# Three casts to ScalarE, ten transposes fewer and another form of one addition, in a graph-attention and quantised-FFN kernel

## The chip, the core and the metric

The kernel runs on one core of a Trainium2 chip. The core has TensorE (PE, matrix products), VectorE (DVE), ScalarE (ACT) and GpSimd (POOL), and SyncE (SP), which here only issues DMAs. PEld is TensorE's weight load, which runs beside its products. The metric is the time of one execution in microseconds of the device; smaller is better. Before the change it is 374.53 us, the median of three runs (374.22 to 374.98).

## What is computed

The input x has 384 rows (nodes) of 1024 features. Two residual blocks follow one another:

```
y = layernorm(x)
q, k, v   = y Wq' + bq,  y Wk' + bk,  y Wv' + bv            1024 x 1024 each
q2,k2,v2  = q Wiq' + biq, k Wik' + bik, v Wiv' + biv        16 heads of 64
mask[s,d] = softplus(edge weight of the edge's type), -inf where there is no edge
attn      = softmax(q2 k2' / 8 + mask)                       per head, 384 x 384
x = x + (attn v2) Wo' + bo

xq   = fake_quant(layernorm(x))          one scale from the largest magnitude
gate = xq quant(Wgate)'                  352 x 1024, a scale for each row
up   = xq quant(Wup)'
h    = fake_quant(silu(gate) * up)       one scale from the largest magnitude
x = x + h quant(Wdown)'                  1024 x 352, a scale for each row
```

quant and fake_quant divide by a scale, round to whole numbers from -128 to 127 and multiply by the scale again. The kernel keeps the whole numbers in bfloat16, multiplies those, and puts the scales back afterwards. The graph-attention block is in float32.

## The kernel before

**Stages.** The span has five parts, by the profile's time. To about 23 us: the layer norm, and the first q blocks. To about 162: the q, k, v and inner-q projections. To about 325: the attention over 8 pairs of heads, with the inner-k and inner-v projections and the quantisation of the FFN weights filled in between. To about 348: the output projection's end, the residual and the second layer norm. Then the FFN.

**The projections.** The weights come in blocks of 128 output features, 512 KB each, two blocks at a time (a pair of blocks, wa and wb, in `project2`). A pair is computed with seven products on halves instead of eight (Strassen's scheme). Each product is `product` (L190), whose four float32 matmuls are eight records in the profile. Around them VectorE makes sums of weights before the products (`left_sums`: L170 s1, L172 s2, L174 the first half of wb; L211, in place, half of wa) and combines the results (L201, L207, L218, L219, L222); ScalarE has two steps for each pair (L204, a copy, and L214, which adds a bias). The second product needs s2 (L172), the sixth needs L211, and a product needs a PSUM buffer that the steps of an earlier one have read out: of four in the projections, of two (`ps_mm`) in the first inner-k pair.

**The mask.** While the projections run, VectorE finds repeated edges (L424 and L431 to L434) and GpSimd scatters the edge values into the mask in DRAM by indirect DMA (L437), four chunks at a time.

**The FFN weights.** `ffn_weights` takes the weights in 14 units: three gate blocks (128, 128 and 96 rows of 1024), three up blocks of the same sizes, and eight down blocks (128 rows of 352). Each unit is loaded by SP (L533) into one of three `row` buffers, so a load waits until the scaling of the unit three before has read its row. `quantise_rows` then takes the row maximum (VectorE, L512), the scale (L513) and its reciprocal (L515), scales to int8 (ScalarE, L518, into the single buffer `w8b`) and casts to bfloat16 (VectorE, L520, into one of two buffers `wqi`). Later TensorE transposes the block (L550 or L557) and ScalarE copies it to its place (L551, L558, L559).

**What sets the order.** On TensorE, SP and GpSimd the order is the program's. On VectorE and ScalarE it is written out up to the end of the projections and again from the second layer norm; between, and for the FFN weights' steps, a scheduler places the instructions, and puts the first units among the projections' last steps. When an instruction waits, everything behind it on its engine waits.

**The end.** In the FFN, TensorE makes gate and up (L920) and, after them, turns the down scales (L937, eight transposes). VectorE multiplies (L927) and reduces to the largest magnitude (L930, L942). Meanwhile TensorE transposes the identity matrix 17 times (L878, in `keep_busy`; nothing reads the results). Then it turns the column of maxima (`all_max`, L129), VectorE reduces it (L131), takes the reciprocal (L948), and VectorE and ScalarE scale h to int8 (L955, L957) and VectorE casts it (L960). Six groups of three matmuls follow (L969), each read out with its scales by VectorE (L973) into y. GpSimd adds the residual x to the first three (L977), VectorE to the last three (L981), after all six are read out. SP sends each out (L978, L982), 256 KB each.

Of the kernel before, what the change touches and what calls it, by code (L numbers as in the profile page):

```python
# [28 lines left out]
ALU = mybir.AluOpType  # L29
# [6 lines left out]
F = 1024  # L36
# [25 lines left out]
def gnn_ffn_kernel(ctx: ExitStack, tc: tile.TileContext, a: dict, out: bass.AP):  # L62
    nc = tc.nc
# [19 lines left out]
    x = act.tile([P, NT, F], F32, name="actT")  # L83
# [50 lines left out]
    w_scale = ffn.tile([P, 2, 3], F32)  # L134
# [372 lines left out]
    v2 = act.tile([P, NT, F], F32, name="actT")  # L507
    outT = act.tile([P, KC, N], F32, name="actT")

    def quantise_rows(wn, rows, n, scale):  # L510
        mx = small.tile([P, 1], F32, name="wmx")
        nc.vector.tensor_reduce(mx[:rows], wn[:rows, :n], axis=AX.X, op=ALU.max, apply_absolute_value=True)  # L512
        nc.vector.tensor_scalar(scale, mx[:rows], 1.0 / QMAX, None, op0=ALU.mult)  # L513
        rs = small.tile([P, 1], F32, name="wrs")
        nc.vector.reciprocal(rs[:rows], scale)  # L515

        w8b = rows_p.tile([P, F], I8, name="w8b", bufs=1)
        nc.scalar.activation(w8b[:rows, :n], wn[:rows, :n], AF.Copy, scale=rs[:rows])  # L518
        wq = rows_p.tile([P, F], BF16, name="wqi", bufs=2)
        nc.vector.tensor_copy(wq[:rows, :n], w8b[:rows, :n])  # L520
        return wq

    def ffn_weights():

        units = [(name, m, ic) for m, name in enumerate(("L0_ffn_w_gate", "L0_ffn_w_up")) for ic in range(3)]
        units += [("L0_ffn_w_down", 2, c) for c in range(KC)]
        ahead = []

        def load_row():
            name, m, j = units[len(ahead)]  # L530
            i0, rows = ICS[j] if m < 2 else (j * P, P)
            wn = rows_p.tile([P, F], F32, name="row")
            nc.sync.dma_start(wn[:rows, : F if m < 2 else I], a[name][i0 : i0 + rows, :])  # L533
            ahead.append(wn)

        load_row()
        load_row()
        yield
        for u, (name, m, j) in enumerate(units):
            wn = ahead[u]  # L540
            if len(ahead) < len(units):
                load_row()
            if m < 2:
                i0, rows = ICS[j]
                wT = (wgT, wuT)[m]
                wq = quantise_rows(wn, rows, F, w_scale[:rows, m, j : j + 1])
                yield
                pt = ps_tp.tile([P, KC, P], BF16, name="tp")
                for k in range(KC):
                    nc.tensor.transpose(pt[:, k, :rows], wq[:rows, k * P : (k + 1) * P], ident_b[:rows, :rows])  # L550
                nc.scalar.copy(wT[:, :, i0 : i0 + rows], pt[:, :, :rows])  # L551
            else:
                wq = quantise_rows(wn, P, I, wd_scale[:, j : j + 1])
                yield
                pt = ps_tp.tile([P, 3, P], BF16, name="tp")
                for ic, (i0, rows) in enumerate(ICS):
                    nc.tensor.transpose(pt[:rows, ic, :], wq[:, i0 : i0 + rows], ident_b)  # L557
                nc.scalar.copy(wdT[:, 0:2, j * P : (j + 1) * P], pt[:, 0:2, :])  # L558
                nc.scalar.copy(wdT[:96, 2, j * P : (j + 1) * P], pt[:96, 2, :])  # L559

    prep = ffn_weights()

    next(prep)
    nc.sync.dma_start(biv_b, row_bcast(a["L0_gnn_biv"], F))

    with ExitStack() as ph:
# [19 lines left out]
        def inner_v(c):  # L586

            cs = slice(c * 256, (c + 1) * 256)
            wt = []
            for j in range(2):  # L590
                wt.append(w.tile([P, F], F32, name="wt"))
                nc.sync.dma_start(
                    wt[j].rearrange("p (k o) -> p k o", k=HK),
                    a["wiv"][j * HK : (j + 1) * HK, :, cs].rearrange("k p o -> p k o"),
                )

            def steps():
                for t in range(NT):
                    pm = ps_mm.tile([P, 256], F32, name="mm")
                    for k in range(KC):  # L600
                        k0 = k % HK * 256
                        nc.tensor.matmul(  # L602
                            pm, vT[:, k, t * P : (t + 1) * P], wt[k // HK][:, k0 : k0 + 256],
                            start=(k == 0), stop=(k == KC - 1),
                        )
                        if k < KC - 1:
                            yield
                    nc.vector.tensor_add(v2[:, t, cs], pm, biv_b[:, cs])
                    yield

            return steps()
# [58 lines left out]
        def out_group(wo, t, g, ks, pm):  # L670
            gs = slice(g * 512, (g + 1) * 512)
            for k in ks:
                nc.tensor.matmul(  # L673
                    pm, outT[:, k, t * P : (t + 1) * P], wo[k][:, gs], start=(k == 0), stop=(k == KC - 1)
                )
                yield
# [11 lines left out]
        for p in range(NP):  # L688
# [4 lines left out]
            if p == NP - 1:  # L693
                early = [(t, g, ps_mm.tile([P, 512], F32, name="mm")) for t, g in ((0, 0), (0, 1))]
                fill, n = (s for t, g, pm in early for s in out_group(wo, t, g, range(NP - 2), pm)), 2 * (NP - 2)
            elif p % 2:
                k2_next, fill = inner_k(p + 1)
                n = 7 * HK + 1
            else:
                fill, n = inner_v(p // 2), NT * KC  # L700
            if p == NP - 2:

                x = act.tile([P, NT, F], F32, name="actT")
# [4 lines left out]
                for t in range(NT):  # L708
                    for g in range(2):
                        gs = slice(g * 512, (g + 1) * 512)  # L710
# [139 lines left out]
    with ExitStack() as ph:  # L850
        ff = ph.enter_context(tc.tile_pool(name="ff", bufs=3))
        ps_x = ph.enter_context(tc.tile_pool(name="ps_x", bufs=4, space=PSUM))
# [21 lines left out]
        def keep_busy(n, pool, name):  # L874

            pt = pool.tile([P, P], F32, name=name)
            for _ in range(n):
                nc.tensor.transpose(pt, ident, ident)  # L878
# [34 lines left out]
        for col, ic, c0, width in ((0, 0, 0, N), (1, 1, 0, N), (2, 2, 0, N // 2), (3, 2, N // 2, N // 2)):  # L913
            i0, rows = ICS[ic]
# [18 lines left out]
        for g in range(2):  # L933
# [2 lines left out]
                c = 4 * g + j  # L936
                nc.tensor.transpose(pt[:, j, :], wd_scale[:, c : c + 1].to_broadcast([P, P]), ident)  # L937
            nc.scalar.copy(wd_scale_b[:, g * 512 : (g + 1) * 512], pt.rearrange("p a b -> p (a b)"))
        keep_busy(17, ps_x, "x")
        mx = small.tile([P, 1], F32, name="hmax")  # L940
        scaled = small.tile([P, 4], F32, name="hscaled")
        nc.vector.tensor_tensor_reduce(  # L942
# [18 lines left out]
        last = []  # L961
        for t in range(NT):
            ts = slice(t * P, (t + 1) * P)
            for g in range(2):
                gs = slice(g * 512, (g + 1) * 512)
# [6 lines left out]
                y = ff.tile([P, 512], F32, name="y", bufs=6)  # L972
# [4 lines left out]
                    nc.gpsimd.tensor_add(y, x[:, t, gs], y)  # L977
                    nc.sync.dma_start(out[t * P : (t + 1) * P, gs], y)  # L978

        for t, gs, y in last:  # L980
            nc.vector.tensor_add(y, x[:, t, gs], y)  # L981
            nc.sync.dma_start(out[t * P : (t + 1) * P, gs], y)  # L982


# [45 lines left out]
```

## Time and profile before

| | |
|---|---|
| median of three runs | 374.53 us (374.22 to 374.98) |
| the profiled execution's own time | 375.57 us |
| its span, first to last instruction | 372.7 us |
| mean granted clock of TensorE | 0.995 |
| TensorE busy | 359.5 us, 96% |
| VectorE busy | 257.1 us, 69% |
| ScalarE busy | 115.5 us, 31% |
| GpSimd busy | 76.0 us, 20% |

A line of the timeline gives the start, the length, the engine, the line in the code, the operation, the output and the inputs, the count, and in square brackets how long the engine was idle before it and what it waited for. Pipelined instructions overlap a little, so the pitch from one start to the next is shorter than the length shown. A line of the stretches ("139.50:164.50") gives the length of the stretch, the busy time of TensorE, its weight load, VectorE, ScalarE and GpSimd, each with a count, then the granted clock of TensorE, the busy share of the DMA engines, and GB/s.

### The profile page before, as it was taken

To read this page: it belongs to the slowest core of one execution; us is meant where nothing else is said; L and a number is where in the kernel's file an instruction comes from. 1 tells how busy PE (TensorE), PEld (TensorE's weight loads), DVE (VectorE), ACT (ScalarE), POOL (GpSimd) and SP (SyncE) were. 2 spreads that over 40 slices of the span, in tenths; PEclk is the share of its full clock that TensorE was granted. 3 is DMA by queue.
4 is the path that set the end of the run, shared out by engine and by line. 5 is a ranking of instruction groups with operands and counts; after the bars stand their busy time and mean duration, and the time that the engine had idled before them with its cause. 6 is when DMAs were issued, how large, how long until landed. Compare 5 with 4: busy or idle time off the path is not lost.

```text
span 372.7 us, 5875 instructions
## 1 busy us (share of the span) xinstructions
PE 359.5 (96%) x2112; PEld 299.9 (80%) x2113; DVE 257.1 (69%) x785; ACT 115.5 (31%) x275; POOL 76.0 (20%) x81
## 2 busy tenths in 40 slices
PE   8999999999999999989999999999999999999981
PEld 8999999999999998888887868686866545449660
DVE  5788878888889969986497357717492621099665
ACT  2352110000000003023482556445444533033630
POOL 6010355455444543430000000000000000000003
PEclk9999999999999999999999999999999999999998
DMA  7969333443333377551170040050294000000004
GB/s 234 393 249 371 130 115 113 116 134 115 113 113 115 113 267 224 176 152 68 38 233 15 19 133 20 21 170 0 96 381 130 36 0 2 0 0 4 0 0 169
DMA packets 17804, 44.50 MB, mean 119 GB/s; under 512 B 3262, under 2 KB 8400, under 8 KB 17392
## 3 DMA queue, kind: packets, MB, share of 16 engines
q1 hardware_dynamic: 15104, 39.46, 31.4%
q0 software_dynamic: 2672, 4.68, 3.9%
q8 instruction: 16, 0.26, 0.3%
q14 instruction: 12, 0.10, 0.1%
HBM read 41.91 MB, written 2.21 MB: 118 GB/s over the span
## 4 chain that ended last, share of the span: by engine, by line
PE 76%; DVE 16%; DMA 3%; ACT 2%; issue 1%; DVEq 0%; POOL 0%; POOLq 0%; ACTq 0%
PE p L190 33%; PE mm L190 8%; PE mm L602 8%; PE tp L655 4%; PE sc L625 3%; PE sc L663 3%; PE mm L673 3%; PE sc L673 3%; PE mm L307 3%; DMA row<-in_L_ffn_w_down_dram 3%; PE tp L315 2%; DVE wmx L512 1%; DVE e L645 1%; DVE st L774 1%; PE mm L920 1%
## 5 line engine op out<-in xcount | busy, mean ns | idle before, releaser
L437 POOL DMA_INDIRECT mask_d<-value,place x51 | 60.5, 1186 | 65.2 <-DVE place L434 45.9
L190 PE MATMUL p<-actT,wt 128*128 128x192 f32 x360 | 66.2, 327 | 1.0 <-DVE wt L211 1.0
L190 PEld LDWEIGHTS p<-actT,wt 128*128 128x128 f32 x360 | 59.5, 190 | 1.8 <-DVE wt L211 1.5
L602 PE MATMUL mm<-wt,actT 128*128 128x256 f32 x192 | 46.1, 384 | 0.0
L602 PEld LDWEIGHTS mm<-wt,actT 128*128 128x128 f32 x192 | 34.8, 190 | 7.8 <-issue 2.2
L635 ACT ACTIVATE e<-s,mn 128x384 f32<-128x384 f32 x48 | 29.0, 605 | 28.2 <-DVE mn L631 28.1
L631 DVE CUSTOM_DVE_ANT_0 s<-sc,mask 128x384 f32<-128x384 f32 x48 | 24.4, 552 | 15.0 <-PE sc L625 14.9
L190 PE MATMUL p<-x_right,s 128*128 128x192 f32 x176 | 32.2, 326 | 0.0
L190 PE MATMUL p<-x_right,wt 128*128 128x192 f32 x176 | 32.2, 326 | 0.0
L855 POOL MEMSET hT<- 128x384 f32 x1 | 0.4, 418 | 154.7 <-PE sc L663 154.7
L190 PEld LDWEIGHTS p<-x_right,s 128*128 128x128 f32 x176 | 29.2, 190 | 0.0
L190 PEld LDWEIGHTS p<-x_right,wt 128*128 128x128 f32 x176 | 29.2, 190 | 0.0
L657 ACT COPY eTs<-tp 128x384 f32<-128x384 f32 x48 | 20.5, 478 | 25.3 <-PE tp L655 25.3
L424 DVE SCALAR_TENSOR_TENSOR junk<-key_b,key,later 128x384 f32<-128x384 f32 (+3 forms) x51 | 27.5, 539 | 0.0
L204 ACT COPY actT<-p 128x192 f32<-128x192 f32 x15 | 4.8, 321 | 64.7 <-PE p L190 64.7
L201 DVE SCALAR_TENSOR_TENSOR actT<-p,bias,actT 128x192 f32<-128x192 f32 x45 | 18.6, 414 | 7.7 <-PE p L190 4.5
L214 ACT ACTIVATE actT<-p,bias 128x192 f32<-128x192 f32 x15 | 6.3, 420 | 50.8 <-PE p L190 29.3
L655 PEld LDWEIGHTS tp<-ident,e 128*128 128x128 f32 x144 | 17.1, 141 | 4.9 <-issue 2.4
L655 PE MATMUL tp<-ident,e 128*128 128x128 f32 x144 | 19.7, 273 | 0.3 <-ACT eTs L657 0.3
L625 PE MATMUL sc<-k,actT 64*128 64x384 f32 x96 | 20.0, 519 | 0.0
L190 PE MATMUL mm<-actT,wt 128*128 128x192 f32 x96 | 19.0, 330 | 0.0
L645 DVE TENSOR_SCALAR e<-e,rs 128x384 f32<-128x384 f32 x48 | 17.2, 415 | 0.4
(220 smaller groups left out, 593.2 us busy)
## 6 DMA issues: line engine op xcount, KB each, us to landing
wt<-in_wq_dram SPq DMA_DIRECT2D x8, 512.0 KB
wt<-in_wk_dram SPq DMA_DIRECT2D x8, 512.0 KB
wt<-in_wv_dram SPq DMA_DIRECT2D x8, 512.0 KB
wt<-in_wiq_dram SPq DMA_DIRECT2D x8, 512.0 KB
wt<-in_wik_dram SPq DMA_DIRECT2D x8, 512.0 KB
wt<-in_wiv_dram SPq DMA_DIRECT2D x8, 512.0 KB
wt<-in_wo_dram SPq DMA_DIRECT2D x8, 512.0 KB
actT<-in_x_dram SPq DMA_DIRECT2D x6, 512.0 KB
```

What stands on the lines that cost most here:

```text
L190: nc.tensor.matmul(z, left[:, k * P : (k + 1) * P], r[:, k, :], start=(k == 0), stop=(k == HK - 1))
L201: nc.vector.scalar_tensor_tensor(dst, z, b, with_, op0=ALU.add, op1=ALU.add)
L424: nc.vector.scalar_tensor_tensor(junk[:, :left], keys[:, (c - k0) * P : (c - k0) * P + left], key[:, c : c + 1], later[:, :left], op0=ALU. ...
L437: ins = nc.gpsimd.indirect_dma_start(out=mask_d, out_offset=bass.IndirectOffsetOnAxis(ap=place[:, c : c + 1], axis=0), in_=value[:, c : c ...
L602: nc.tensor.matmul(pm, vT[:, k, t * P : (t + 1) * P], wt[k // HK][:, k0 : k0 + 256], start=(k == 0), stop=(k == KC - 1),)
L625: nc.tensor.matmul(ps[t, h], q2[hs, t * P : (t + 1) * P], k2[hs, :], start=True, stop=True)
L631: nc.vector.tensor_tensor_reduce(s, ps[t, h], mask[:, t, :], -SCALE, 3.0e38, op0=ALU.add, op1=ALU.min, accum_out=mn[h][:, t : t + 1],)
L635: nc.scalar.activation(e[h][:, t, :], s, AF.Exp, bias=mn[h][:, t : t + 1], scale=-1.0, accum_out=sm[h][:, t : t + 1],)
L645: nc.vector.tensor_scalar(e[h][:, t, :], e[h][:, t, :], rs[:, t : t + 1], None, op0=ALU.mult)
L655: nc.tensor.transpose(pt[:, t * P : (t + 1) * P], e[h][:, t, m * P : (m + 1) * P], ident)
L657: nc.scalar.copy(eT[h][m], pt)
L673: nc.tensor.matmul(pm, outT[:, k, t * P : (t + 1) * P], wo[k][:, gs], start=(k == 0), stop=(k == KC - 1))
```

## The change

Three edits in three places.

The casts: for the first three units, which are the three gate blocks, the cast from int8 to bfloat16 is issued on ScalarE instead of VectorE. The other eleven stay on VectorE.

The transposes of the identity matrix behind gate and up: 7 instead of 17.

The first of the three additions that VectorE makes at the end: x times 1.0 plus y in one scalar_tensor_tensor instead of a tensor_add. The values are the same.

```diff
-    def quantise_rows(wn, rows, n, scale):
+    def quantise_rows(wn, rows, n, scale, on_scalar=False):
...
         nc.scalar.activation(w8b[:rows, :n], wn[:rows, :n], AF.Copy, scale=rs[:rows])
         wq = rows_p.tile([P, F], BF16, name="wqi", bufs=2)
-        nc.vector.tensor_copy(wq[:rows, :n], w8b[:rows, :n])
+        if on_scalar:
+            nc.scalar.copy(wq[:rows, :n], w8b[:rows, :n])
+        else:
+            nc.vector.tensor_copy(wq[:rows, :n], w8b[:rows, :n])
         return wq
...
-                wq = quantise_rows(wn, rows, F, w_scale[:rows, m, j : j + 1])
+
+                wq = quantise_rows(wn, rows, F, w_scale[:rows, m, j : j + 1], on_scalar=u < 3)
...
-        keep_busy(17, ps_x, "x")
+        keep_busy(7, ps_x, "x")
...
-        for t, gs, y in last:
-            nc.vector.tensor_add(y, x[:, t, gs], y)
+        for n, (t, gs, y) in enumerate(last):
+            if n == 0:
+
+                nc.vector.scalar_tensor_tensor(y, x[:, t, gs], 1.0, y, op0=ALU.mult, op1=ALU.add)
+            else:
+                nc.vector.tensor_add(y, x[:, t, gs], y)
             nc.sync.dma_start(out[t * P : (t + 1) * P, gs], y)
```

The scheduler's order changes with it, on VectorE and ScalarE only, and only around the projections' last steps and the first units. On VectorE, the row maximum of the third gate block and that of the first up block stand earlier, both ahead of L172 of the last inner-q pair; the reciprocal of the third gate block stands ahead of that pair's L174; and the maximum of the last up block stands just ahead of L207 of the first inner-k pair instead of just behind it. On ScalarE the scaling of the third gate block moves ahead of L214 of the last inner-q pair, and its cast stands between the first wgT copy and the scaling of the first up block.

## The prediction

> **What bounds the kernel now.** I read the page first, then the timelines of TensorE, VectorE and ScalarE where the casts run, then the timeline and fine windows of the end.
>
> ```profile
> PE 359.5 (96%) x2112; PEld 299.9 (80%) x2113; DVE 257.1 (69%) x785; ACT 115.5 (31%) x275; POOL 76.0 (20%) x81
> ...
> 139.50:164.50 25.00, 23.61 (x141) 22.48 (x140) 24.78 (x68) 5.14 (x8) 10.80 (x8) 1.00 0.54 166
> ...
> 148.36 1.57 PE L190 MATMUL p<-actT,wt 128*128 128x192 f32 x8 [0.42 <-DVE wt L211]
> 152.96 1.57 PE L190 MATMUL p<-right,s 128*128 128x192 f32 x8 [0.43 <-DVE s L172]
> 158.96 1.57 PE L190 MATMUL p<-actT,wt 128*128 128x192 f32 x8 [0.53 <-DVE wt L211]
> 167.56 1.57 PE L190 MATMUL mm<-k_right,wt 128*128 128x192 f32 x8 [0.53 <-DVE k L201]
> ...
> 146.70 0.69 DVE L520 CAST wqi<-w8b 128x1024 bf16<-128x1024 int8 x1
> 148.64 0.68 DVE L520 CAST wqi<-w8b 128x1024 bf16<-128x1024 int8 x1
> 153.37 1.20 DVE L512 TENSOR_REDUCE wmx<-row 128x1 f32<-128x1024 f32 x1
> 165.96 1.22 DVE L512 TENSOR_REDUCE wmx<-row 96x1 f32<-96x1024 f32 x1 [0.82 <-DMA row<-in_L_ffn_w_up_dram]
> 160.72 1.15 ACT L518 ACTIVATE w8b<-row,wrs 96x1024 int8<-96x1024 f32 x1 [3.13 <-DVE w_scale L513]
> ...
> 357.42 2.02 PE L878 MATMUL x<-ident 128*128 128x128 f32 x17
> 358.03 0.08 DVE L942 DVE_READ_ACCUMULATOR2_ANT hmax<- 128x1 f32 x1
> 359.27 0.27 PE L129 MATMUL tp<-ident,hmax 128*128 128x128 f32 x1
> 365.27 1.26 POOL L977 TENSOR_TENSOR y<-actT,y 128x512 f32<-128x512 f32 x1
> 365.93 1.15 DVE L981 TENSOR_TENSOR y<-actT,y 128x512 f32<-128x512 f32 x1
> 367.25:367.50 0.25, 0.00 (x0) 0.00 (x0) 0.25 (x1) 0.00 (x0) 0.00 (x0) 1.00 0.43 164
> 369.75:370.00 0.25, 0.00 (x0) 0.00 (x0) 0.00 (x0) 0.00 (x0) 0.00 (x0) 0.50 0.96 385
> ```
>
> TensorE is the bound over the whole span. It lost time where the first two casts run: in the 25 us from 139.5 VectorE is busy for 24.78, and TensorE stops three times there and once just after, each time for VectorE. At the end, the 17 idle transposes run on after VectorE has the maximum ready (358.11); the next transpose, which the chain needs, stands behind them. The last addition group starts slowly: 1.15 us against 0.68 for its two neighbours, while GpSimd's third addition is still running (to 366.53). Then the DMA engines are full from about 367.35 to 370.2.
>
> **Part 1, the casts.** Three int8-to-bf16 casts (gate rows; pitch 0.61 us each on VectorE) go to ScalarE. ScalarE's price is not in the trace. The nearest rows are its 128x1024 copy (bf16, 1.01 us) and its 128x1024 scaling to int8 (1.15 us); the dearest per element, the 128x384 exponential at 0.605 us, would make 1.6 us. The low end is VectorE's own 0.68. I take 1.05, from the copy, which has the same operation and size.
>
> The order of the built program also changes on VectorE. The row maximum of the third gate block and of the first up block move earlier, to before L172 (s2) of the last wiq pair; the third reciprocal comes before that pair's L174, so the third scaling to int8 on ScalarE no longer waits until 160.72 but starts near 153.45. This frees the row buffer, and SP, with only two wik loads ahead of it (their 1 MB passed by 155 before), can fetch the last up block some 7 us sooner. That ends the 0.82 us DMA wait at 165.96.
>
> A product is eight matmul records and takes 1.30 us undisturbed. Walking VectorE's new order with the measured pitches (added values, semaphores about 0.07 us):
> - L207 to 146.10, L170 to 146.70, no cast, L201 to 147.02, L211 to 147.62. TensorE needs L211 at 147.78: the first stop goes.
> - L424 to 148.03, moved maximum (1.13) to 149.16. ScalarE meanwhile does scaling, cast, scaling, and is at L214 by 148.5 as before, so L201 runs to 149.48. L158, L218 and L513 to 150.28.
> - The second moved maximum reads the first up block. Its load is issued at 146.20 as before and its half-microsecond windows show the bytes past by 149.3, so it runs at once, to 151.41. L219, L424, L222 to 152.22, L172 to 152.82. TensorE is there already at 151.68: the second stop stays, longer, and the product starts near 152.87 instead of 152.96. Here the two saved casts (1.22) are spent on the moved maximum (1.13).
> - After it VectorE has that maximum behind it: L174 to 154.57, L201 to 157.17, L211 to 157.77. TensorE asks at 158.18: the third stop goes.
> - The second up block's maximum runs 159.51 to 160.64, the last one's 163.11 to 164.24 without a wait; L207 ends 164.51, before TensorE asks for its PSUM buffer at 164.68; L201 to 165.2, before 165.98: the fourth stop goes.
> TensorE so ends the first wik pair at 169.88 instead of 171.79.
>
> As a check: a stop costs its gap and a slow restart. Start to start, the four cost 0.69, 0.70, 0.80 and 1.03, together 3.22 us; after, one of about 1.3 is left. Gain 1.9.
>
> The third cast is off the path on VectorE (its idle before is 0.45). On ScalarE it stands behind the first wgT copy and ahead of the scaling of the first up block: that scaling ends near 179.2 instead of 180.07, since all is 1.9 earlier and the cast takes 1.05. The first w_down row then lands at 181.45 by the 2.25 us of the chain's row; the row maximum on VectorE waits for it and the next scaling ends at 182.55 instead of 184.73. Nothing TensorE needs is later than its 1.9. From there to the end TensorE is nearly dense (72.89 of 73.00 us from 195 to 268), loads are started by finished work, and the gain should carry through. ScalarE has the room: 5.14 of 25 us busy. Bounds: 0.7 (the last stop stays and the exponential's rate holds on ScalarE) to 2.3 (the small TensorE gap at 192.5 goes too). I take -1.9.
>
> **Part 2, ten transposes fewer.** Their pitch is 1.85/17 = 0.109 us, so 1.09. With seven, TensorE is free at 358.07; the maximum, read out at 358.11, reaches it near 358.17 (row_max took 0.06 earlier). The weight load of L129, at 359.16, starts there: -1.0. What is late next is VectorE's reduction chain. Behind L129 all follows at once (L131, L948, L955, L960, L969), GpSimd and the output DMAs with it. Bounds -1.09 and 0. [...]
>
> **Part 3, the addition as scalar_tensor_tensor.** Its own price is 0.06 over the plain add (0.74 against 0.68 in L973 and L981). Whether it also stands still beside GpSimd no row shows: L973, not slowed under GpSimd, reads one operand from PSUM; this one reads both from SBUF, as the slowed add does. If it runs free, VectorE ends 0.41 earlier (next start 366.59 for 367.00); if not, 0.06 later. The chain of waits would book that on the path. I book 0: from 367.35 the DMA engines carry four 256 KB blocks without a pause, some 0.7 us each, beginning with GpSimd's third, issued at 366.56. The first block from VectorE is queued behind that one on SP, and the last is already issued (368.3) while the engines still work off earlier ones. Bounds -0.2 and +0.06.
>
> [...]
>
> **Sum.** -1.9 - 1.0 + 0 = -2.9. The profiled execution took 375.57 (span 372.7 and 2.87 around it), so 372.7; it lies 1.04 above the median of the runs, 374.53, which becomes **371.6**.
>
> **Rivals.**
> - *The full list of gains*: the new form runs free and the last blocks follow it, and the gap at 192.5 goes: -1.9 - 0.15 - 1.0 - 0.2 = -3.25, 371.3. For it: the chain of waits; against: the full DMA windows. I keep it in the likeliest case's own range, 370.9 to 372.2.
> - *Half of part 1*: a row maximum moved earlier meets a row not yet landed, or ScalarE's cast takes 1.6 and delays L214 and so L201, and a stop is back. Each stop costs 0.7 to 1.0: -0.9 - 1.0 = -1.9, 372.6. Against: 1 us of slack on the landing, 0.5 on L214.
> - *The maximum is not ready*: part 2 gives only what VectorE's reduction allows, say half. -2.4, 372.1. Against: 358.11 is read from the trace.
> [...]
>
> [...]
> - *No change seen*: the path returns the time at a later wait, 374.5. Little speaks for it.
>
> **How the numbers follow.** Forecast with the first rival 0.62, half of part 1 0.14, part 2 halved 0.07, slower by clock or a wait that I don't see 0.12, none 0.05. The measurement tells about 0.2% (0.7 us) from no change. Faster 0.83, same 0.05, slower 0.12. The range takes the first three: 370.7 (all gains, less 0.2 of spread) to 373.2 (part 1 at its lower bound 0.7, part 2 whole, rounded up).
>
> **What would show it.** In the profile after: TensorE's rows with waits for L211 near 148 and 158 and for L201 near 167 gone, the one for L172 near 152.9 still there; no DMA wait at the last up maximum; the three casts on ScalarE near 1.05 us; the attention's first L602 group near 169.9; L878 x7, with the weight load of L129 right after the maximum; clock 1.00 through L969; the first last addition either 0.74 or near 1.2 us, with no difference to the end; span near 369.8. It is wrong if VectorE stops at a row maximum for a DMA, if the time gained by 170 is given back before 268, or if the clock falls before 361.

## The result, and the profile after

The changed kernel takes 371.59 us, the median of six runs (370.62 to 372.53); six runs of the kernel before beside them gave 374.29 (373.26 to 374.98). The ratio is 0.9931, with a 95% interval from 0.9913 to 0.9949: 2.6 us faster (1.9 to 3.3). The forecast was 371.6, 2.9 us below the 374.53 that three runs had given for the kernel before.

The profiled execution is the slowest of the six: 372.53 us, span 370.8 (before 375.57 and 372.7). Of the 3.04 us between the two executions 1.14 lie outside the spans (2.87 around the span before, 1.73 after) and say nothing of the change; 1.9 lie inside.

The page of the changed kernel, the stretch from 139.5 to 164.5 (columns as before), then the timeline of TensorE, ScalarE and VectorE there:

```profile
PE 357.4 (96%) x2102; PEld 298.6 (81%) x2103; DVE 255.3 (69%) x782; ACT 118.2 (32%) x278; POOL 72.7 (20%) x81
...
139.50:164.50 25.00, 23.33 (x140) 22.32 (x139) 23.91 (x68) 7.10 (x10) 7.96 (x8) 1.00 0.66 205
...
142.19 1.57 PE L190 MATMUL p<-actT,wt 128*128 128x192 f32 x8 [0.54 <-DVE actT L201]
154.35 1.57 PE L190 MATMUL p<-right,s 128*128 128x192 f32 x8 [1.01 <-DVE s L172]
...
147.61 1.04 ACT L521 CAST wqi<-w8b 128x1024 bf16<-128x1024 int8 x1
154.92 1.15 ACT L518 ACTIVATE w8b<-row,wrs 96x1024 int8<-96x1024 f32 x1 [1.23 <-DVE w_scale L513]
...
140.59 1.22 DVE L512 TENSOR_REDUCE wmx<-row 128x1 f32<-128x1024 f32 x1 [2.54 <-DMA row<-in_L_ffn_w_gate_dram]
149.44 1.21 DVE L512 TENSOR_REDUCE wmx<-row 96x1 f32<-96x1024 f32 x1
151.69 1.20 DVE L512 TENSOR_REDUCE wmx<-row 128x1 f32<-128x1024 f32 x1
153.62 0.68 DVE L172 TENSOR_TENSOR s<-s,wt 128x512 f32<-128x512 f32 x1
```

The three stops that were to go are gone, and the one for s2 is there, 1.01 long. The two row maxima moved ahead of L172 are seen just before it. The casts are on ScalarE, 1.04 us each, and the third scaling starts at 154.92 instead of 160.72. One thing was not forecast: a stop of 0.54 us at 142.19, because VectorE waited 2.54 us for the first gate row (before: 1.57, and no stop).

The end, from the timeline, and two fine windows (length, five engines, granted clock, DMA share, GB/s):

```profile
356.44 0.93 PE L882 MATMUL x<-ident 128*128 128x128 f32 x7
357.06 0.08 DVE L946 DVE_READ_ACCUMULATOR2_ANT hmax<- 128x1 f32 x1
357.26 0.13 PEld L129 LDWEIGHTS tp<-ident,hmax 128*128 128x128 f32 x1
360.85 3.72 POOL L981 TENSOR_TENSOR y<-actT,y 128x512 f32<-128x512 f32 x3 [15.20 <-DVE y L977]
363.97 1.15 DVE L987 SCALAR_TENSOR_TENSOR y<-actT,y 128x512 f32<-128x512 f32 x1
365.04 1.28 DVE L989 TENSOR_TENSOR y<-actT,y 128x512 f32<-128x512 f32 x2
...
367.50:368.00 0.50, 0.00 (x0) 0.00 (x0) 0.00 (x0) 0.00 (x0) 0.00 (x0) 0.50 0.99 373
368.00:368.50 0.50, 0.00 (x0) 0.00 (x0) 0.00 (x0) 0.00 (x0) 0.00 (x0) 0.50 0.39 143
```

L129's weight load follows the maximum by 0.12 us. The addition in its new form takes the 1.15 us that the plain one took: GpSimd's third addition runs to 364.57. The DMA engines are again full until just past 368, long after VectorE's last addition.

Ahead of the last products (L969 before, L973 after) TensorE is idle, in the kernel before from 359.54 to 361.33. Before, then after:

```profile
361.33 0.60 PE L969 MATMUL mm<-wdT,hq 128*128 128x512 bf16 x2 [1.79 <-DVE hq L960]
...
359.38 0.60 PE L973 MATMUL mm<-wdT,hq 128*128 128x512 bf16 x2 [1.79 <-DVE hq L964]
```

**A table by stage.** The profiles of the experiments can be laid beside each other by five landmarks: start of the s2 product near 133; start of the s2 product of the last inner-q pair (152.96 before); the attention's first group (L602 before); the first of the eight transposes of the down scales (L937 before); the weight load of L129; the end of the span. Each column is the time from one to the next in us.

```
                       133-s2   s2-attention   -scales    -L129    -end
before                 19.70       18.83       184.75     2.62    13.54
only the seven         19.70       18.76       184.43     1.69    13.48
only the form          19.60       18.97       184.57     2.62    13.60
only the casts         19.67       17.08       184.49     2.63    13.55
two casts              20.58       17.09       184.97     2.62    13.56
changed, first         20.66       17.09       184.13     1.69    13.54
changed, again         19.52       17.08       184.45     1.69    13.53
no transposes          20.03       17.08       184.44     1.69    13.49
operand in PSUM        19.67       17.08       184.23     1.68    13.53
two rows early         19.90       17.08       184.83     1.69    13.52
three rows early       18.97       17.09       184.41     1.69    13.52
later maxima           18.97       17.09       184.08     1.69    13.47
later, two rows        20.28       17.08       184.38     1.69    13.50
later, three rows      18.20       16.98       184.27     1.69    13.53
```

The second, fourth and fifth columns hardly move except by the edit that acts on them. The third has a scatter of 0.9. The first one moves by itself, from 19.52 to 20.66 in two executions of the same kernel, and the experiments go after it.

### The profile page after: what moved, and what is told of

The parts are those of the page before. It is cut to its first block, busy times and chain, and to the rows that moved or that the text cites. A ratio compares the mean times of both kernels' runs of the same rounds, so it can differ in the third digit from the quotient of the medians.

```text
span 370.8 us, 5857 instructions
## 1 busy us (share of the span) xinstructions
PE 357.4 (96%) x2102; PEld 298.6 (81%) x2103; DVE 255.3 (69%) x782; ACT 118.2 (32%) x278; POOL 72.7 (20%) x81
## 4 chain that ended last, share of the span: by engine, by line
PE 80%; DVE 12%; DMA 4%; issue 1%; ACT 1%; SPq 1%; DVEq 0%; ACTq 0%
PE p L190 32%; PE mm L190 10%; PE mm L606 10%; PE sc L629 5%; PE tp L659 4%; PE sc L667 4%; PE mm L677 3%; PE sc L677 3%; PE mm L307 3%; DMA wt<-in_wq_dram 3%; DMA row<-in_L_ffn_w_gate_dram 2%; DVE st L778 1%; PE mm L924 1%; DVE y L977 1%; PE x L924 1%
## 5 line engine op out<-in xcount | busy, mean ns | idle before, releaser
L437 POOL DMA_INDIRECT mask_d<-value,place x51 | 57.2, 1122 | 68.4 <-DVE place L434 47.9
L201 DVE SCALAR_TENSOR_TENSOR actT<-p,bias,actT 128x192 f32<-128x192 f32 x45 | 18.7, 415 | 7.6 <-PE p L190 4.7
L214 ACT ACTIVATE actT<-p,bias 128x192 f32<-128x192 f32 x15 | 6.3, 420 | 49.1 <-PE p L190 27.6
L612 DVE TENSOR_TENSOR actT<-mm,biv_b 128x256 f32<-128x256 f32 x12 | 5.1, 422 | 18.9 <-PE mm L606 18.8
```

Of the source, the lines that this page charges most:

```text
L201: nc.vector.scalar_tensor_tensor(dst, z, b, with_, op0=ALU.add, op1=ALU.add)
L437: ins = nc.gpsimd.indirect_dma_start(out=mask_d, out_offset=bass.IndirectOffsetOnAxis(ap=place[:, c : c + 1], axis=0), in_=value[:, c : c ...
```

## The experiments

Differences are the ratio against the kernel before on the same chip, less one, times its median (374.14 us; 374.23 for the two casts, the operand and the two kernels with three rows early), with the 95% interval in brackets. A profile is of one execution, which can lie anywhere in the spread of its kernel's runs.

**Each part alone, and the whole again.** The first kernel has only the casts' edit, the second only `keep_busy(7, ...)`, the third only the scalar_tensor_tensor.

```diff
+wq = quantise_rows(wn, rows, F, w_scale[:rows, m, j : j + 1], on_scalar=u < 3)   # first alone
+keep_busy(7, ps_x, "x")                                                          # second alone
+nc.vector.scalar_tensor_tensor(y, x[:, t, gs], 1.0, y, op0=ALU.mult, op1=ALU.add)  # third alone
```

> Only the three casts on ScalarE, with the order on VectorE that comes with it; 17 transposes and the plain addition stay. Theory of the prediction: -1.9 us beside the kernel before (range -1.2 to -2.3), because three of the four stops of TensorE between 148 and 168 us go and the one for s2 (L172) stays, about 1.2 us long. Rival (the gain is luck of landing DMAs, since the first gate row landed at different times in the two profiles): -0.5 to 0. Rival (ScalarE becomes the wait): 0 or slower.

Measured: 372.86 us, -1.2 (-1.8 to -0.6); two thirds of the -1.9. In its profile the casts do all that they were to do: only the stop for s2 is left, 1.30 long, and the attention starts at 169.63. But this execution is the fastest of the twelve (372.07), so the profile shows more gain than the median. The kernel has the casts together with the scheduler's new order; no run has the casts on ScalarE in VectorE's old order, so the two are not told apart.

> Only 7 transposes instead of 17 behind gate and up. Theory: -1.0 us; the weight load of the transpose of the maxima starts about 0.1 us after the maximum is read out, the granted clock stays 1.00 through the last matmuls. Rival (the clock falls in the idle stretch in some executions): a wider spread, some runs 2 us or more above the others, and a mean gain under 0.5 us.

Measured: 372.89 us, -1.0 (-1.5 to -0.5). The four stops stay as before, and L129's weight load stands 0.12 us behind the end of the maximum's read:

```profile
357.82 0.08 DVE L942 DVE_READ_ACCUMULATOR2_ANT hmax<- 128x1 f32 x1
358.02 0.13 PEld L129 LDWEIGHTS tp<-ident,hmax 128*128 128x128 f32 x1
```

> Only the first last addition as scalar_tensor_tensor. Theory: 0.0 us (within 0.15); the instruction takes 1.15 us like the plain add, because it stands still until GpSimd's third addition has ended. Rival (the chain of waits is right and the form runs free): 0.74 us long and the end 0.4 us earlier.

Measured: 373.97 us, +0.1 (-0.5 to +0.8). The addition is 1.15 long in this profile as well.

> The changed kernel once more, beside its three parts on the same chip. Theory: -2.9 us, the sum of the three parts run alone within 0.4 us. Rival (the parts share a wait): 0.5 us or more less than the sum.

Measured: 371.18 us, -2.8 (-3.5 to -2.0). Here the wait for the first gate row was 0.66, there was no stop near 142, and the attention started at 169.63 against 171.44 in the first profile. So the same program gives the forecast stretch in one execution and loses 1.1 us of it in another. The parts alone add up to -2.1 by their ratios; the 0.7 to the whole's -2.8 is within their intervals, but more than the 0.4 that was expected.

**Two casts only.** The third cast goes back to VectorE, in the kernel before.

```diff
+wq = quantise_rows(wn, rows, F, w_scale[:rows, m, j : j + 1], on_scalar=u < 2)
```

> The kernel before with the casts of the first two gate blocks alone on ScalarE, the third on VectorE. Theory (the gain of the casts comes from the first two, which lie in the 25 us in which VectorE is full; the third lies where VectorE has idle time): as with all three casts alone, -1.2 us against the kernel before, within 0.4, with the first three matmuls of the attention's scores near 169.6 and the stops for L211 and L201 gone. Rival (the third cast carries a good part, because the scaling of the first up block then comes sooner): -0.6 or less.

Measured: 373.23 us, -0.9 (-1.3 to -0.5): within the theory's range, though the interval reaches to the rival's -0.6. The stops for L211 and the last L201 are gone with two casts alone, and the column from s2 to the attention is the same 17.09. Its first three score matmuls came late (attention at 170.95), because in this profile the wait for the first gate row was 2.46 and the stop near 142 was back.

**No transposes at all.** The changed kernel with none behind gate and up.

```diff
-        keep_busy(7, ps_x, "x")
+        keep_busy(0, ps_x, "x")
```

> The changed kernel with no transposes at all behind gate and up, instead of 7. Theory: about -2.9 us beside the kernel before, no more than the changed kernel, because the transpose of the maxima waits for VectorE's maximum and not for TensorE; the weight load starts where it starts with 7. Rival (each transpose costs its 0.109 us all the way down): -3.6 us. Rival (TensorE's clock falls, with about 0.8 us more idle before the 1.8 us): some executions 2 us or more above the others, and slower than with 7.

Measured: 371.63 us, -2.6 (-3.4 to -1.8), no better than with seven. The time from the scales to L129 is 1.69 with seven and with none: VectorE's reduction decides. The bracket below names ScalarE's copies of the down scales (two of 0.59, the first from 354.86). But the load starts at 355.91, while the second copy still runs (to 355.93), and the first, whose PSUM buffer is the next in turn for this transpose, was over by 355.45. What came last is the maximum, read out by 355.79. The granted clock stayed at 1.00 from 355 to 361, with TensorE busy for only 0.55 us from 355 to 357:

```profile
355.71 0.08 DVE L946 DVE_READ_ACCUMULATOR2_ANT hmax<- 128x1 f32 x1
355.91 0.13 PEld L129 LDWEIGHTS tp<-ident,hmax 128*128 128x128 f32 x1 [0.90 <-ACT wd_scale_b L942]
...
355.00:357.00 2.00, 0.55 (x4) 0.15 (x2) 1.38 (x7) 1.14 (x3) 0.00 (x0) 1.00 0.00 0
357.00:359.00 2.00, 0.98 (x5) 0.60 (x7) 1.70 (x5) 0.92 (x2) 0.00 (x0) 1.00 0.00 0
```

**The operand of the late addition.** The first of VectorE's additions reads its second operand from PSUM.

```diff
-                nc.vector.scalar_tensor_tensor(y, x[:, t, gs], 1.0, y, op0=ALU.mult, op1=ALU.add)
+                nc.vector.scalar_tensor_tensor(y, x[:, t, gs], 1.0, pm, op0=ALU.mult, op1=ALU.add)
```

> The changed kernel, where the first late addition takes its second operand from the PSUM bank of its product instead of from y. It leaves out the two scales of that one output block, so the block is not the reference's; the work on every other engine is unchanged. Theory (VectorE stands still beside GpSimd because both operands of the addition are in SBUF): the addition takes about 0.74 us, as the other instructions of this form that read PSUM, instead of 1.15, and VectorE's next addition starts some 0.4 us sooner. The end does not move: the DMA engines are full from about 365.5 to 368.2 whatever VectorE does, so -2.8 against the kernel before, the changed kernel's own figure, within 0.15. Rival (the chain of waits, by which the additions are on the path): the end comes 0.4 us sooner, -3.2. Rival (the form itself, or the bank, is what costs 1.15 us here): the addition stays at 1.15.

Measured: 371.56 us, -2.7 (-3.4 to -2.0). The timeline and two windows of this kernel:

```profile
358.95 3.72 POOL L981 TENSOR_TENSOR y<-actT,y 128x512 f32<-128x512 f32 x3 [15.19 <-DVE y L977]
362.08 0.68 DVE L987 SCALAR_TENSOR_TENSOR y<-actT,x 128x512 f32<-128x512 f32 x1
362.67 1.29 DVE L989 TENSOR_TENSOR y<-actT,y 128x512 f32<-128x512 f32 x2
...
365.50:366.00 0.50, 0.00 (x0) 0.00 (x0) 0.00 (x0) 0.00 (x0) 0.00 (x0) 0.50 1.03 389
366.00:366.50 0.50, 0.00 (x0) 0.00 (x0) 0.00 (x0) 0.00 (x0) 0.00 (x0) 0.50 0.60 225
```

The same instruction beside the same addition of GpSimd (it runs to 362.67) takes 0.68 instead of 1.15 when one operand is in PSUM, and VectorE's next addition starts 0.59 after it instead of 1.07. Yet from L129 to the end it is 13.53 us, as in the changed kernel (13.53 and 13.54): 0.48 us of VectorE's time at the end of the chain of waits are worth nothing, since the output DMAs fill the engines behind it.

**What moves the first column.** Two candidates: the landing of the gate rows, and the row maxima ahead of L172. The first edit issues the first two gate rows ahead of the inner-k weight blocks on SP; the second orders the maxima of the three up blocks behind the last combine of the first inner-k pair; then both.

```diff
+            if todo[i + 1][0] == "wik":                       # rows early: two, or all three of ICS
+                for i0, rows in ICS[:2]:
+                    wn = rows_p.tile([P, F], F32, name="row")
+                    nc.sync.dma_start(wn[:rows], a["L0_ffn_w_gate"][i0 : i0 + rows, :])
+                    first_rows.append(wn)
...
-        ahead = []
+        ahead = list(first_rows)
...
-        load_row()
-        load_row()
...
+        if after is not None:                                 # later maxima, for u > 2
+            tc.add_manual_dep(first.ins, after.ins.name, order, reason="behind the first inner-k pair")
```

> The changed kernel with the row maxima of the three up blocks ordered behind the first inner-k pair on VectorE. Theory (VectorE's in-order work is what stops TensorE, and the stop at L172 comes from the moved maximum): that stop shrinks from 1.2 us to under 0.2 and none comes back; -4.0 us beside the kernel before. Rival (the third stop comes back in its place, since VectorE is still full): -3.2. Rival (the later maxima delay the weights of up or the attention's first scores): -2.9 or less.

Measured: 370.24 us, -4.1 (-4.8 to -3.4), as expected. TensorE does not stop for s2 any more (the product starts 0.12 us late), though VectorE still waited 1.91 us for the first gate row. Without the maxima ahead of L172 a landing as late as this costs TensorE only late starts, 0.77 us in the first column (18.97; the last kernel below has none and takes 18.20). With them, a wait of 1.54 came with a stop of 1.01 (the kernel with the operand in PSUM).

> The changed kernel with the loads of the first two gate rows issued by SP ahead of the two inner-k weight blocks instead of behind them. Theory (the 1.3 to 2.5 us that VectorE waits for the first gate row is passed on to TensorE): VectorE waits for no gate row, the stop at L172 shrinks from 1.2 us to under 0.3, and the spread of the times gets smaller; -4.0 us beside the kernel before. Rival (that wait is covered): -2.9, and the same spread.

Measured: 372.22 us, -2.0 (-2.8 to -1.2): a miss, half of what was expected and no better than the changed kernel. SP's queue and VectorE's timeline show why:

```profile
123.35 0.90 SPq L481 DMA_DIRECT2D row<-in_L_ffn_w_gate_dram  x2
139.87 1.68 SPq L600 DMA_DIRECT2D wt<-in_wiv_dram  x2
141.60 0.49 SPq L542 DMA_DIRECT2D row<-in_L_ffn_w_gate_dram  x1
...
148.16 1.22 DVE L518 TENSOR_REDUCE wmx<-row 96x1 f32<-96x1024 f32 x1 [1.66 <-DMA row<-in_L_ffn_w_gate_dram]
```

The first two rows are there in time. The third is issued at 141.60, behind two inner-v weight blocks, and VectorE now waits 1.66 us for that one. The wait had only moved to the next row in the same queue, and s2 came 1.53 us late.

> Both of the last two edits. Theory: 23 products from 138.5 us on run without a stop, 1.30 us each, so the attention starts 3.4 us earlier than before; -4.4 us beside the kernel before. Rival (the two edits remove different waits and their gains add): -5.1.

Measured: 371.13 us, -3.3 (-4.0 to -2.5): a miss too, by the same mechanism: the third gate row is waited for 3.09 us, and TensorE stops at 150.68 and 152.95, with no row maximum of an up block ahead of L172. So a row that lands late enough stops TensorE by itself. It is worse than the later maxima alone.

The last two kernels load all three gate rows early, without and with the later maxima.

> The changed kernel with all three gate rows loaded ahead of the inner-k weight blocks (the earlier run had only two of them there, and VectorE then waited 1.66 us for the third, with TensorE's stop for s2 still there). Theory (there are two separate causes of TensorE's stops: rows that have not landed, and the two row maxima ahead of L172 of the last inner-q pair): no row maximum of a gate block waits for a DMA, and the stop near 142 is gone; the stop for s2 (L172) stays at about 1.0 us, since two row maxima still stand ahead of it, now those of two up blocks. Some 0.5 us better than the changed kernel: -3.2 against the kernel before. Rival (the landing of the rows is the only cause): no stop left, -4.1 or better.

Measured: 371.28 us, -3.1 (-3.9 to -2.4). No gate row is waited for and the stop near 142 is gone; the stop for s2 stays, at 0.61 rather than 1.0. But VectorE now waits for the first up row:

```profile
147.67 1.22 DVE L518 TENSOR_REDUCE wmx<-row 128x1 f32<-128x1024 f32 x1 [0.73 <-DMA row<-in_L_ffn_w_up_dram]
...
152.59 1.57 PE L190 MATMUL p<-right,s 128*128 128x192 f32 x8 [0.61 <-DVE s L172]
```

Without these 0.73 us, L172 would end near 151.80 (an estimate: it ran from 151.85 for 0.68), and TensorE asks for s2 at 151.81, a product's 1.30 behind the start of the one before (150.51). So this run does not refute the rival that the landing of rows is the only cause. The later maxima alone do: there the stop went although a row landed late. That late rows are a cause too is shown by the run with both edits, above. The gain over the changed kernel is not told apart by the times, but the first column, 18.97, is lower than in any run with late rows and early maxima.

> Both: all three gate rows loaded ahead of the inner-k weight blocks, and the row maxima of the three up blocks behind the last combine of the first inner-k pair. Theory (two causes, both removed): no DMA wait at a gate row's maximum and no stop of TensorE between 138 and 170; the run with the later maxima alone gave -4.1, and its small late starts, together about 0.5 us, go too: -4.6 against the kernel before. Rival (the later maxima alone already have all there is, as TensorE did not stop in that run): -4.1. Rival (moving 1.4 MB of rows ahead of the inner-k weights makes those late): a new wait for the weight blocks, and less than -4.1.

Measured: 369.55 us, -4.7 (-5.4 to -4.0), the fastest kernel of all and as the theory said. TensorE is full for the whole 25 us, with VectorE at 20.17:

```profile
139.50:164.50 25.00, 25.00 (x156) 25.00 (x155) 20.17 (x57) 5.14 (x8) 9.92 (x10) 1.00 0.64 203
...
150.33 1.46 PE L190 MATMUL p<-actT,wt 128*128 128x192 f32 x8
151.63 1.46 PE L190 MATMUL p<-right,s 128*128 128x192 f32 x8
```

From the s2 product near 133 to the attention there are 27 products; at the undisturbed 1.30 us that is 35.1, and this kernel takes 35.18.

## Why the prediction was right or wrong, step by step

- *The third and fourth stops go.* Right. From the s2 product to the attention the walk gave 17.01 us (152.87 to 169.88), and 17.08 or 17.09 was measured in every kernel with the casts moved and the scheduler's own order, against 18.83 before: -1.75, where -1.82 was forecast.
- *The first stop goes, the second stays and grows; together about nothing (-0.09).* The signs are right, the size is not steady. In the kernels with the casts moved and the scheduler's own order, the first column moved by -0.18 to -0.03 in three profiles (first gate row waited for 0.66 to 1.54 us), by +0.88 and +0.96 in two (2.46 and 2.54), and by +0.33 in the one without transposes, where the first row was waited for only 1.04, but the third 0.78, and the stop for s2 was 1.66. The step that failed is the start of the walk: it took VectorE's state at the first gate row's maximum, with its wait of 1.57, as given. A wait of 2.46 or 2.54 us exhausted the slack, and TensorE stopped near 142, for 0.46 and 0.54. Among the signs of a wrong forecast stood a stop of VectorE at a row maximum for a DMA. It came: longer than before at the first gate row, whose maximum the change had not moved, in two of the six profiles, and at the third, whose maximum it had moved, in three others.
- *Slack of 1 us on the landing of moved rows.* Half right. The first up row was never waited for in the changed kernel. The third gate row, whose maximum moved too, was waited for 0.65 us in the second profile of the changed kernel, 0.39 in that of the casts alone and 0.78 in that without transposes, and the stop for s2 was 1.16, 1.30 and 1.66 there. The walk had asked only of the up row whether it lands in time.
- *Part 1 as a sum, -1.9 (bounds -0.7 to -2.3).* The bounds held; the value is the best of the executions (-1.93 in the two first columns of the second profile, -0.78 in those of the first). Alone it measured -1.2 (-1.8 to -0.6). Whether a late row costs the kernel before as much can't be told: no profile of its order has one (1.46 to 1.57).
- *The casts' price, 1.05 us on ScalarE.* Right: 1.03 to 1.05 in all profiles.
- *The gain carries through to the end.* Right, within the scatter of the third column: 184.75 before and from 184.08 to 184.97 in the others, which no edit explains and which I leave open. The third cast did what the walk said: in the first profile the two scalings behind it end at 180.80 and 184.11, 9.36 and 12.67 behind the attention's start (171.44), where the forecast had 9.32 and 12.67 (179.2 and 182.55 behind 169.88).
- *Part 2, -1.0.* -0.93 in the profiles (2.62 to 1.69), the same without any transposes; alone -1.0. L129's weight load waits for the maximum alone: it starts 0.12 us behind it with seven and with none.
- *Part 3, 0.* Right, and for the reason given: time saved there does not reach the end (0.48 us saved with the operand in PSUM, and 13.53 us from L129 to the end as before that edit). Whether the form stands still beside GpSimd was left open; with both operands in SBUF it takes 1.15 us there, as the plain addition does.
- *The clock.* 1.00 through the last matmuls (L969 before, L973 after) and through the idle stretch ahead of them, in every profile. The forecast's 0.12 for slower counts a fall of the clock among its causes; no run shows one ahead of the last matmuls, neither with 17 transposes nor with seven nor with none. The 1.79 us in the two lines of the result is 0.2 too long: the record of the first of the 18 last matmuls is missing in those two profiles. Where all 18 are there, TensorE is idle for 1.56 (1.57 in one).
- *Span near 369.8.* 370.8 in the first profile, 369.3 in the second; the gap between them lies for the most part in the first column.

The mechanism is right in parts 2 and 3 and in the last two stops of part 1. That the total came out at 371.59 for 371.6 is in part luck. Part 1 was overstated (-1.2 alone for -1.9), the six runs lie 1.9 us apart, and the kernel before came out 0.24 lower beside them than in the three runs that the forecast started from, so that -2.6 was measured for -2.9. The range's upper end is loose too: its own terms, -0.7 and -1.0, give 372.8, and 373.2 stands there.

## What to carry to other kernels

A saved instruction on a full engine is worth the stops that it ends, and a scheduler may spend it at once on another: here two casts saved (1.22 us) paid for a row maximum (1.13) that keeps the stop for s2, and ordering that maximum later gave as much as the casts. When a walk through an engine's order starts from a DMA wait of the profile, take that wait as a spread (here 0.66 to 2.54 us), and look for the next load in the same queue before moving one load forward. A chain of waits that ends in an instruction says nothing of what its time is worth while the DMA queue behind it is full (here 0.48 us were worth nothing).

## What the runs showed of the hardware

The granted clock fell to 0.50 only after the last matmul, but not at a fixed distance: read from quarter-microsecond windows, 1.89 us after its end in the first profile of the changed kernel, 2.90 in the second, 3.95 before, and up to 5.0 in the fourteen profiles. What sets the distance no run here shows. The idle stretch of 1.56 us ahead of the last products is only 0.33 shorter than the shortest of them, though none of the fourteen profiles shows a fall there.

In the ten profiles in which SP issues the first gate row behind the inner-k weight blocks, VectorE waited 0.66 to 2.54 us for it, in programs whose order up to there is the same. From SP's first issue of the gate rows to VectorE's start on the first of them it was 5.74 to 7.39 us, so it is the landing that moves. What moves it no run here shows.
